# Row tiles of 2 rows by 16 columns in the sums of an involution, with paired weight groups and a ring of 38 rows

## The chip, the cores and the metric

The kernel runs on one core of a Trainium2 chip. The time is the device time of that core in microseconds (us), the median over runs. Durations, waits and rates come from one execution that the hardware profiler recorded. TensorE is PE in the profile (its weight loads are PEld), VectorE is DVE, ScalarE is ACT, GpSimd is POOL and SyncE is SP.

## The reference

Two layers on x of shape (32, 256, 32, 32), each with a group normalization ahead of it and a residual addition behind it. The first is a 3x3 convolution on values rounded to half precision, the second an involution: a 7x7 filter whose 49 weights are computed anew for each pixel and for each of 16 groups of 16 channels.

```python
# layer 0
x = x + (float_quantize(patches3x3(gn(x)) @ weight.T) + bias)      # operands quantized too
# layer 1, on v = gn(x)
y   = relu(bn(einsum('oc,bchw->bohw', w1, v)))                     # 64 channels
w   = einsum('oc,bchw->bohw', w2, y) + b2                          # 16 groups * 49 taps
w   = w.reshape(b, G, K * K, H, W)
out = einsum('bgkhw,bgckhw->bgchw', w, patches7x7(v))              # a filter of its own per pixel and group
x   = x + out
```

## The kernel before

Images go through one after the other, but several are under way at once. The outer loop counts steps `n`; an image takes `per = 16` of them in its last part, the sums. Everything of an image that comes ahead of its sums (both normalizations, the convolution, y, the transposed pixels) is a generator `front(b)` that starts 56 steps earlier and advances a stage in each step. So a step holds stages of some three images' fronts, and in every second step a call of `sums` (L501), `add_windows` (L523) and `weights` (L402). The order on each engine is the order in which the loop writes the instructions (`manual_schedule`); the framework adds the semaphores. In a pair of steps PE runs the sums of one tile, the weights of another image and half a unit of convolution (9 matmuls, L332).

The convolution is done as nine shifted matmuls in float16 for each half of the channels. `weights` computes, for four rows of the image, the 49 filter weights of each pixel and group by float32 matmuls (L410) into two PSUM tiles; DVE adds the bias and writes them into `w_sb` (L428), a ring of 24 rows in SBUF. As the weights of an output pixel have to reach the source pixels around it, an eviction writes the seven rows of taps into seven rows of the ring; where the ring's end or the image's edge cuts a row off, `ring_pieces` (L438) splits the write into several instructions.

`scatter` (L466) writes eight rows of the ring to `wd` in DRAM, one transfer for each column of taps, shifted so that `wd` holds, by source pixel, what that pixel contributes to the window of outputs around it. `load_bands` (L479) fetches from `wd` a band for each tile of 8 rows: 16 transfers, of which POOL issues 14 and SP 2, into one of three band buffers.

In `sums` the source pixels of half a tile are the contraction of a matmul: the pixels (transposed) are the stationary side and the band the moving one. A tile of sums is 4 rows by 16 columns, 64 source pixels; two of them lie in the two halves of PE's rows, and four groups' results in four strips of 32 columns. The result of a tile is a window of 10 rows (`WIN = XR + K1 - 1`) by 19 columns, so 190 columns of PSUM. A call handles two row tiles, two halves of the channels, two groups of a pair and four strips: 32 products. Each float32 product is two weight loads and two matmuls in the profile. `add_windows` (L523) adds the windows to x in SBUF, one instruction for each row tile, written one step after the sums. The accumulators alternate by side: the left and right half of the image have an `acc` each, of two banks.

What the prediction speaks of by line: L332 convolution, L380 y (`py`), L395 transposes (`pt`), L410 weights, L428 their evictions, L477 scatter, L490 bands, L515 sums, L531 additions.

Of the kernel before, what the change touches and what calls it, by code (L numbers as in the profile page):

```python
# [9 lines left out]
F32 = mybir.dt.float32  # L10
AF = mybir.ActivationFunctionType
ALU = mybir.AluOpType

P = 128
B, C, H, W = 32, 256, 32, 32
N = H * W
NT = 512
RT = NT // W
CH = C // P
K0, PAD0 = 3, 1  # L20
K1, PAD1 = 7, 3
TAPS = K1 * K1
CR = 64
G = 16
# [9 lines left out]

XR = 4
RG = 2
KP = P // RG
TR = RG * XR  # L40
SIDES = 2
JC = W // SIDES
K = H // TR
M = K * SIDES
WIN = XR + K1 - 1
WINC = JC + K1 - 1
WINI = JC + PAD1

WB = G * WIN
WPIX = K1 * WB + XR
SW = K1 * G
S = H + 2 * PAD1
T = 4
TW = P // T
PAIR = 3 * GC
PAIRS = G // 2
ROW = S * WPIX  # L60
WR = 4
NBAND = 3
SHARE = 8
NPIX = 6
RING = 24
FRONT = -56
LOAD = -63
LEAD = 18
# [3 lines left out]
def tile_quant_conv_then_involution(  # L72
# [16 lines left out]
    nc = tc.nc  # L89
    PSUM = bass.MemoryType.PSUM  # L90

    const = ctx.enter_context(tc.tile_pool(name="const", bufs=1))
# [45 lines left out]
        nc.gpsimd.memset(t, 0.0)  # L138

    y_sb = [const.tile([P, N // 2], F32, name=f"y_{i}") for i in range(2)]  # L140
    bands = [const.tile([P, SIDES, WINC * WB + XR], F32, name=f"band_{i}") for i in range(NBAND)]
    for t in bands[CH:]:
        nc.gpsimd.memset(t, 0.0)
    pixels = [const.tile([P, 2, PAIRS, PAIR], F32, name=f"pixels_{i}") for i in range(NPIX)]
# [1 line left out]
        nc.gpsimd.memset(t, 0.0)  # L146


    w_sb = const.tile([P, 2, RING, G, WIN], F32, name="w_sb")
    wd = dram.tile([H, S, WPIX], F32, name="wd")  # L150
    acc = [ps_acc.tile([P, RG, NT], F32, name=f"acc_{d}") for d in range(SIDES)]

    wq = const.tile([P, CH, K0 * K0, C], F16, name="wq")
    staged = []
# [4 lines left out]
    w2_sb = const.tile([P, K1, SW], F32, name="w2_sb")  # L159
    for i in range(2):  # L160
        nc.sync.dma_start(w2_sb[i * CR : (i + 1) * CR], w2)
    b2_sb = const.tile([P, 2, SW], F32, name="b2_sb")
    for dj in range(K1):
        t, e = divmod(dj, 2)
        nc.sync.dma_start(b2_sb[t * TW : (t + 1) * TW, e], b2[dj].partition_broadcast(TW))

    bias_sb = const.tile([P, CH], F32, name="bias_sb")
    nc.sync.dma_start(bias_sb, bias0.rearrange("(h p) -> p h", p=P))
# [15 lines left out]


    for col, cols, at, n in (
        (0, S, K1 * WB, XR),
        (PAD1, PAD1, 0, PAD1 * WB),
        (W, PAD1, (K1 - PAD1) * WB, PAD1 * WB),
    ):  # L190
        to = bass.AP(
            tensor=wd.tensor,
            offset=wd.offset + col * WPIX + at,
            ap=[[ROW, H], [WPIX, cols], [1, n]],
        )
        nc.sync.dma_start(to, bands[NBAND - 1][:H, 0, :n].unsqueeze(1).to_broadcast([H, cols, n]))
# [205 lines left out]
    def weights(b, r0):  # L402

        pws = [ps_w.tile([P, 2, 2, SW], F32, tag=f"pw{i}", name=f"pw{i}") for i in range(2)]
        for r in range(2):
            for t in range(T):
                for i in range(2):
                    half = slice(i * CR, (i + 1) * CR)
                    dj = slice(2 * t, min(2 * t + 2, K1))
                    nc.tensor.matmul(  # L410
                        pws[i][t * TW : (t + 1) * TW, r, : dj.stop - dj.start],
                        y_sb[b % 2][half, (r0 // 2 + r) * W : (r0 // 2 + r + 1) * W],
                        w2_sb[half, dj],
                        start=True,
                        stop=True,
                    )
        for i in range(2):
            for e in range(2):
                p = P if e == 0 else (K1 // 2) * TW
                for r, rows, d0, d1, at in ring_pieces(b, r0 + 2 * i):  # L420

                    to = w_sb[:p, e]
                    to = bass.AP(
                        tensor=to.tensor,
                        offset=to.offset + at * WB + K1 - 1 - d0,
                        ap=[to.ap[0], [WB, rows], [WB - 1, d1 - d0], [WIN, G]],
                    )
                    nc.vector.tensor_tensor(  # L428
                        to,
                        pws[i][:p, r : r + rows, e, d0 * G : d1 * G].rearrange("p r (d g) -> p r d g", g=G),  # L430
                        b2_sb[:p, e, d0 * G : d1 * G]
                        .unsqueeze(1)
                        .to_broadcast([p, rows, (d1 - d0) * G])
                        .rearrange("p r (d g) -> p r d g", g=G),
                        ALU.add,
                    )

    def ring_pieces(b, r0):  # L438

        def place(r, d):
            s = r0 + r + d - PAD1
            return (b * H + s) % RING if 0 <= s < H else None

        def together(d):
            return place(0, d) is not None and place(1, d) == place(0, d) + 1

        pieces = []
        for rows, ok in (  # L450
            ((0, 2), together),
            ((0, 1), lambda d: place(0, d) is not None and not together(d)),
            ((1, 1), lambda d: place(1, d) is not None and not together(d)),
        ):
            d = 0
            while d < K1:
                d0 = d
                while d < K1 and ok(d) and place(rows[0], d) == place(rows[0], d0) + d - d0:
                    d += 1
                if d > d0:  # L460
                    pieces.append((*rows, d0, d, place(rows[0], d0)))
                else:
                    d += 1
        return pieces

    def scatter(b, k, part):  # L466

        at = (b * H + k * TR) % RING
        for dj in range(part, K1, 2):
            t, e = divmod(dj, 2)  # L470
            to = bass.AP(
                tensor=wd.tensor,
                offset=wd.offset + k * TR * ROW + dj * WPIX + (K1 - 1 - dj) * WB,
                ap=[[WPIX, TW], [ROW, TR], [1, WB]],
            )
            rows = w_sb[t * TW : (t + 1) * TW, e, at : at + TR]
            nc.sync.dma_start(to, rows.rearrange("p s g r -> p s (g r)"))  # L477

    def load_bands(b, k):  # L479

        band = bands[(b * K + k) % NBAND]
        for i in range(JC):
            j = i // 2 + i % 2 * JC // 2
            src = bass.AP(
                tensor=wd.tensor,
                offset=wd.offset + k * TR * ROW + (j + PAD1) * WPIX,
                ap=[[ROW - 1, TR], [JC * WPIX, SIDES], [1, WPIX]],
            )
            queue = nc.sync if i % SHARE == SHARE - 1 else nc.gpsimd
            queue.dma_start(band[j::JC, :, j * WB : j * WB + WPIX], src)  # L490

    def windows(b, m):


        k, d = divmod(m, SIDES)
        for g in range(RG):
            top = k * TR + g * XR - PAD1
            at = acc[d][:, g, : CH * WINI * WIN].rearrange("p (h j r) -> p h j r", h=CH, r=WIN)
            yield g, at, top, max(top, 0), min(top + WIN, H)

    def sums(b, m):  # L501

        k, d = divmod(m, SIDES)
        j0 = 0 if d else PAD1
        band = bands[(b * K + k) % NBAND][:, d]
        px = pixels[(b * K + k) % NPIX][:, d]
        for h in range(CH):
            for v in range(2):
                for g, at, top, f, l in windows(b, m):
                    p = slice(g * KP, (g + 1) * KP)  # L510
                    of = band[p, g * XR + j0 * WB : g * XR + (j0 + WINI) * WB]
                    of = of.rearrange("p (j g r) -> p j g r", g=G, r=WIN)
                    for t in range(T):
                        a = h * T + t
                        nc.tensor.matmul(  # L515
                            at[t * TW : (t + 1) * TW, h, :, f - top : l - top],
                            px[p, a, v * GC : v * GC + TW],
                            of[:, :, 2 * a + v, f - top : l - top],
                            start=(h, v) == (0, 0),
                            stop=(h, v) == (CH - 1, 1),  # L520
                        )

    def add_windows(b, m):  # L523

        d = m % SIDES
        to = x_tiles[b].rearrange("p h (r c) -> p h r c", c=W)
        j0 = d * (JC - PAD1)
        for g, at, top, f, l in windows(b, m):
            x_at = to[:, :, f:l, j0 : j0 + WINI]
            of = at.rearrange("p h j r -> p h r j")[:, :, f - top : l - top]  # L530
            nc.vector.tensor_tensor(x_at, of, x_at, ALU.add)  # L531
# [10 lines left out]
    def due(n, lag):  # L542

        b, i = divmod(n - lag, per)
        return (b, i) if 0 <= b < B else (None, None)

    with tc.manual_schedule():
        fronts = {}
        for n in range(FRONT, B * per + 2):
            b, i = due(n, FRONT)  # L550
# [12 lines left out]
            b, i = due(n, 0)  # L563
            if b is not None and i % 2 == 0:
                sums(b, i // 2)
            b, i = due(n, 1)
            if b is not None and i % 2 == 0:
                add_windows(b, i // 2)
                if i // 2 == M - 1:
                    store(b, 1)  # L570
                    x_tiles.pop(b)
# [58 lines left out]
```

## Time and profile before

| | |
|---|---|
| median of 3 runs | 1392.44 us (1381.25 to 1393.82) |
| span of the profiled execution, its own time from the first to the last instruction | 1387.9 us |
| first and last start of L515, the sums | 97.4 and 1382.2 us |
| instructions | 70,012 |
| PE busy | 1250.5 us (90%), 29,440 matmuls and 29,440 weight loads |
| DVE busy | 934.7 us (67%) |
| ACT busy | 727.6 us (52%) |
| POOL busy | 1007.6 us (73%) |
| DMA | 369.33 MB in 366,232 packets, mean 266 GB/s |
| mean granted TensorE clock | 0.981 |

The profiled execution has no time of its own other than its span; it lies within the range of the three runs. In the lines below, a group reads: line, engine, operation, out<-in, partitions by elements, count, then busy us and mean ns of one, then the engine's idle time just ahead of it and what ended it. "issue" means that the profile shows nothing that the engine waited for. A row of the timeline reads: start us, length us, and what ran. The DMA row has a digit for each fortieth of the span, in tenths of the 16 engines.

### The profile page before, as it was taken

The numbers are of one execution on the slowest core, as the hardware profiler recorded it, in microseconds if no ns is written. First come the engines' busy times: TensorE is split into PE (matmuls) and PEld (weight loads), VectorE is DVE, ScalarE is ACT, GpSimd is POOL, SyncE is SP. The second block draws the span as 40 slices with busy tenths as digits, with TensorE's granted clock in tenths as the row PEclk, the third lists the DMA queues.
The fourth block names the chain that finished last, engine by engine and source line by source line (L and its number), as shares of the span: only waits on it lengthen the run. The fifth ranks groups of instructions, "written<-read, shape, count | busy, mean of one in ns | idle before, by whom it ended". The sixth has DMA issues, their size and how long they took to land.

```text
span 1387.9 us, 70012 instructions
## 1 busy us (share of the span) xinstructions
PE 1250.5 (90%) x29440; PEld 798.5 (58%) x29440; DVE 934.7 (67%) x3179; ACT 727.6 (52%) x1699; POOL 1007.6 (73%) x1818
## 2 busy tenths in 40 slices
PE   2899999899899999998899999899999999999665
PEld 1356555566565665655565666566566655666543
DVE  4467776677767776776576677667777776677652
ACT  4866555465645555655455555545565654653300
POOL 8057777777787777767777787776876777778785
PEclk9999999999999999999999999999999999999986
DMA  6079999999999998999999999999999999999995
GB/s 217 1 195 286 283 277 283 284 266 292 287 277 274 287 294 254 285 279 269 273 275 286 289 275 279 288 277 264 288 283 272 295 285 279 280 280 272 280 269 162
DMA packets 366232, 369.33 MB, mean 266 GB/s; under 512 B 78624, under 2 KB 308192, under 8 KB 365664
## 3 DMA queue, kind: packets, MB, share of 16 engines
q1 hardware_dynamic: 279904, 235.72, 57.5%
q0 software_dynamic: 86016, 129.14, 33.8%
q8 instruction: 234, 3.83, 1.2%
q14 instruction: 78, 0.64, 0.1%
HBM read 183.81 MB, written 180.74 MB: 263 GB/s over the span
## 4 chain that ended last, share of the span: by engine, by line
PE 55%; DMA 25%; DVE 5%; issue 5%; POOL 4%; SPq 3%; ACT 3%; POOLq 0%; DVEq 0%; ACTq 0%
PE pc L332 22%; PE acc L515 17%; DMA band<-wd 14%; PE pw L410 10%; DMA wd<-w_sb 8%; POOL band L490 4%; PE py L380 3%; DVE w_sb L428 3%; SPq L477 3%; PE pt L395 2%; DMA out<-x 1%; ACT junk L219 1%; DVE x L531 1%; DMA band<-in_w 1%; ACT xn L278 0%
## 5 line engine op out<-in xcount | busy, mean ns | idle before, releaser
L490 POOL DMA_DIRECT2D band<-wd x1792 | 978.0, 548 | 364.1 <-DMA band<-wd 225.3
L428 DVE TENSOR_TENSOR w_sb<-pw,b_sb 128x16 f32<-128x16 f32 (+9 forms) x1920 | 455.5, 349 | 359.2 <-PE pw L410 345.4
L332 PE MATMUL pc<-xq,wq 128*128 128x496 f16 (+3 forms) x2304 | 536.4, 379 | 32.5 <-ACT xq L278 28.0
L515 PE MATMUL acc<-band,pixels 64*32 64x190 f32 (+1 forms) x16384 | 411.6, 322 | 80.2 <-DMA band<-wd 44.6
L332 PEld LDWEIGHTS <-wq 128*128 128x128 f16 x2304 | 206.8, 98 | 328.2 <-issue 113.0
L515 PEld LDWEIGHTS acc<-band,pixels 64*32 64x32 f32 x16384 | 296.1, 108 | 165.1 <-issue 100.1
L410 PE MATMUL pw<-w_sb,y 64*32 64x224 f32 (+1 forms) x8192 | 291.2, 332 | 15.1 <-issue 13.9
L531 DVE TENSOR_TENSOR x<-acc,x 128x380 f32<-128x380 f32 (+1 forms) x512 | 261.7, 511 | 33.6 <-PE acc L515 24.6
L410 PEld LDWEIGHTS pw<-w_sb,y 64*32 64x32 f32 x8192 | 180.6, 106 | 45.7 <-issue 28.8
L399 ACT COPY pixels<-pt 128x512 f32<-128x512 f32 x128 | 73.6, 575 | 224.0 <-PE pt L395 224.0
L219 ACT ACTIVATE junk<-x 128x512 f16<-128x512 f32 (+1 forms) x192 | 146.5, 763 | 18.0 <-DVE x L348 9.6
L219 ACT ACTIVATE junk<-x,mean 128x1024 f16<-128x1024 f32 x128 | 147.1, 1149 | 4.3
L250 ACT ACTIVATE s<-back,eps 128x2 f32<-128x2 f32 x64 | 18.9, 296 | 207.3 <-DVE back L235 207.2
L346 DVE TENSOR_SCALAR q<-pc 128x512 f16<-128x512 f32 x128 | 87.2, 682 | 19.2 <-PE pc L332 19.0
L278 ACT ACTIVATE xn<-x,off,rstd 128x512 f32<-128x512 f32 x128 | 96.1, 800 | 0.0
L348 DVE SCALAR_TENSOR_TENSOR x<-q,bias_sb,x 128x512 f32<-128x512 f16 x128 | 92.0, 719 | 0.2
L395 PEld LDWEIGHTS pt<-ident,xn 128*128 128x128 f32 x512 | 63.9, 142 | 27.7 <-issue 3.3
L395 PE MATMUL pt<-ident,xn 128*128 128x128 f32 x512 | 78.0, 275 | 1.5 <-ACT pixels L399 1.5
L240 ACT ACTIVATE mean<-back 128x2 f32<-128x2 f32 x64 | 12.7, 198 | 120.6 <-DVE back L235 120.6
L278 ACT ACTIVATE xq<-x,off,rstd 128x1024 f16<-128x1024 f32 x64 | 75.5, 1226 | 0.0
L380 PEld LDWEIGHTS py<-xn,w_sb 128*64 128x64 f32 x2048 | 62.7, 138 | 16.7 <-issue 8.3
L380 PE MATMUL py<-xn,w_sb 128*64 128x64 f32 x2048 | 67.5, 224 | 2.8 <-ACT xn L278 1.8
(40 smaller groups left out, 374.5 us busy)
## 6 DMA issues: line engine op xcount, KB each, us to landing
wd<-w_sb SPq DMA_DIRECT2D x896, 160.0 KB
band<-wd POOLq DMA_DIRECT2D x1792, 70.2 KB, 4.9
x<-in_x SPq DMA_DIRECT2D x64, 512.0 KB
out<-x SPq DMA_DIRECT2D x64, 512.0 KB
band<-wd SPq DMA_DIRECT2D x256, 70.2 KB
band<-in_w SPq DMA_DIRECT2D x2, 1152.0 KB
w_sb<-in_w SPq DMA_DIRECT2D x2, 196.0 KB
wd<-band SPq DMA_DIRECT2D x2, 180.0 KB
```

Of the source, the lines that this page charges most:

```text
L219: nc.scalar.activation(junk[:, n0:n1], src[:, h, n0:n1], func, bias=bias, accum_out=self.sums[:, i : i + 1])
L278: nc.scalar.activation(dst, src, AF.Identity, bias=self.off[:, one], scale=self.rstd[:, one])
L332: nc.tensor.matmul(pc.rearrange("p (r c) -> p r c", c=W)[:, r0 - nt * RT : r1 - nt * RT, c0:c1], wq[:, kh, k, mh * P : (mh + 1) * P], xq[: ...
L346: nc.vector.tensor_scalar(q, pc, F16_MAX, -F16_MAX, ALU.min, ALU.max)
L348: nc.vector.scalar_tensor_tensor(xt[:, mh, cols], q, bias_sb[:, mh : mh + 1], xt[:, mh, cols], ALU.add, ALU.add)
L380: nc.tensor.matmul(py[i * CR : (i + 1) * CR, cols], w1_sb[:, kh, :], px[:, r : r + 2], start=kh == 0, stop=kh == CH - 1,)
L395: nc.tensor.transpose(pt[:, i, h * P : (h + 1) * P], xn[:, h, (m + i) * P : (m + i + 1) * P], ident)
L410: nc.tensor.matmul(pws[i][t * TW : (t + 1) * TW, r, : dj.stop - dj.start], y_sb[b % 2][half, (r0 // 2 + r) * W : (r0 // 2 + r + 1) * W], w ...
L428: nc.vector.tensor_tensor(to, pws[i][:p, r : r + rows, e, d0 * G : d1 * G].rearrange("p r (d g) -> p r d g", g=G), b2_sb[:p, e, d0 * G : d ...
L490: queue.dma_start(band[j::JC, :, j * WB : j * WB + WPIX], src)
L515: nc.tensor.matmul(at[t * TW : (t + 1) * TW, h, :, f - top : l - top], px[p, a, v * GC : v * GC + TW], of[:, :, 2 * a + v, f - top : l - top],
L531: nc.vector.tensor_tensor(x_at, of, x_at, ALU.add)
```

## The change

A tile of sums becomes 2 rows by 16 columns (`XR = 2`), and four of them (`RG = 4`) lie in the four quarters of PE's rows with 32 source pixels each. The window shrinks to 8 rows, 152 columns of PSUM, and a call has 64 products. Each row tile has an accumulator bank of its own, `acc[g]`, which both sides share. `add_windows` has four instructions of 8-row windows, and is called right behind `sums` in the same step.

The weights are laid out in pairs of groups (`V = 2`, `A = 8`): the two groups of a pair are neighbours in `w_sb`, in `wd` and in the bands, and w2 and b2 are permuted on the host to match. A pixel's row in `wd` holds 7 x 128 values and a pad of 12 (before 7 x 160 and 4).

The ring has 38 rows, an image's 32 and three on either side, at fixed places. So an eviction always writes all seven rows of taps, those outside the image too, in one instruction of two image rows by 16 groups by 7 taps; `ring_pieces` goes. The matmuls of `weights` write with the tap column ahead of the row, and the bias is held twice, once for each of the two rows.

```diff
-XR = 4
-RG = 2
+XR = 2
+RG = 4
...
+V = 2
+A = G // V
 WB = G * WIN
-WPIX = K1 * WB + XR
+PAD = V * (TR - XR)
+WPIX = K1 * WB + PAD
...
-RING = 24
+RING = H + 2 * PAD1
...
-    w_sb = const.tile([P, 2, RING, G, WIN], F32, name="w_sb")
+    w_sb = const.tile([P, 2, RING, A, WIN, V], F32, name="w_sb")
-    acc = [ps_acc.tile([P, RG, NT], F32, name=f"acc_{d}") for d in range(SIDES)]
+    acc = [ps_acc.tile([P, NT], F32, name=f"acc_{g}") for g in range(RG)]
...
-    b2_sb = const.tile([P, 2, SW], F32, name="b2_sb")
+    b2_sb = const.tile([P, 2, 2, SW], F32, name="b2_sb")
     for dj in range(K1):
         t, e = divmod(dj, 2)
-        nc.sync.dma_start(b2_sb[t * TW : (t + 1) * TW, e], b2[dj].partition_broadcast(TW))
+        for r in range(2):
+            nc.sync.dma_start(b2_sb[t * TW : (t + 1) * TW, e, r], b2[dj].partition_broadcast(TW))
...
-                        pws[i][t * TW : (t + 1) * TW, r, : dj.stop - dj.start],
+                        pws[i][t * TW : (t + 1) * TW, : dj.stop - dj.start, r],
...
-                for r, rows, d0, d1, at in ring_pieces(b, r0 + 2 * i):
...
+                evict(pws[i][:p, e], e, 0, 2, 0, K1, r0 + 2 * i)
+
+    def evict(of, e, r, rows, d0, d1, at):
+
+        p = of.shape[0]
+        to = w_sb[:p, e]
+        to = bass.AP(
+            tensor=to.tensor,
+            offset=to.offset + at * WB + V * (K1 - 1 - d0),
+            ap=[to.ap[0], [V * WIN, rows * A], [WB - V, d1 - d0], [1, V]],
+        )
+        of = of.rearrange("p r (a d v) -> p (r a) d v", a=A, v=V)
+        bias = b2_sb[:p, e, r : r + rows].rearrange("p r (a d v) -> p (r a) d v", a=A, v=V)
+        nc.vector.tensor_tensor(to, of[:, :, d0:d1], bias[:, :, d0:d1], ALU.add)
...
-        at = (b * H + k * TR) % RING
+        at = k * TR + PAD1
...
-                ap=[[ROW - 1, TR], [JC * WPIX, SIDES], [1, WPIX]],
+                ap=[[ROW - V, TR], [JC * WPIX, SIDES], [1, WPIX]],
...
-            at = acc[d][:, g, : CH * WINI * WIN].rearrange("p (h j r) -> p h j r", h=CH, r=WIN)
+            at = acc[g][:, : CH * WINI * WIN].rearrange("p (h j r) -> p h j r", h=CH, r=WIN)
...
-                    of = band[p, g * XR + j0 * WB : g * XR + (j0 + WINI) * WB]
-                    of = of.rearrange("p (j g r) -> p j g r", g=G, r=WIN)
+                    of = band[p, V * g * XR + j0 * WB : V * g * XR + (j0 + WINI) * WB]
+                    of = of.rearrange("p (j a r v) -> p j a r v", a=A, r=WIN, v=V)
...
-                            of[:, :, 2 * a + v, f - top : l - top],
+                            of[:, :, a, f - top : l - top, v],
...
                 sums(b, i // 2)
+                add_windows(b, i // 2)
             b, i = due(n, 1)
             if b is not None and i % 2 == 0:
-                add_windows(b, i // 2)
                 if i // 2 == M - 1:
                     store(b, 1)
```

More of the change, by code (lines that the diff above doesn't have):

```diff
@@ L140, in tile_quant_conv_then_involution @@
     y_sb = [const.tile([P, N // 2], F32, name=f"y_{i}") for i in range(2)]
-    bands = [const.tile([P, SIDES, WINC * WB + XR], F32, name=f"band_{i}") for i in range(NBAND)]
+    bands = [const.tile([P, SIDES, WINC * WB + PAD], F32, name=f"band_{i}") for i in range(NBAND)]
     for t in bands[CH:]:
@@ L186, in tile_quant_conv_then_involution @@
     for col, cols, at, n in (
-        (0, S, K1 * WB, XR),
+        (0, S, K1 * WB, PAD),
         (PAD1, PAD1, 0, PAD1 * WB),
@@ L419, in weights @@
                 p = P if e == 0 else (K1 // 2) * TW
-                for r, rows, d0, d1, at in ring_pieces(b, r0 + 2 * i):
[L422 to L464, printed above, removed]
+                evict(pws[i][:p, e], e, 0, 2, 0, K1, r0 + 2 * i)
@@ L476, in scatter @@
             rows = w_sb[t * TW : (t + 1) * TW, e, at : at + TR]
-            nc.sync.dma_start(to, rows.rearrange("p s g r -> p s (g r)"))
+            nc.sync.dma_start(to, rows.rearrange("p s a r v -> p s (a r v)"))
     def load_bands(b, k):
@@ L603 @@
     v = {name: np.asarray(a) for name, a in inputs.items()}
-    w2 = v["L1_conv_w2"].reshape(G, K1, K1, CR).transpose(3, 2, 1, 0).reshape(CR, K1, K1 * G)
-    b2 = v["L1_conv_b2"].reshape(G, K1, K1).transpose(2, 1, 0).reshape(K1, K1 * G)
+    w2 = v["L1_conv_w2"].reshape(A, V, K1, K1, CR).transpose(4, 3, 0, 2, 1).reshape(CR, K1, K1 * G)
+    b2 = v["L1_conv_b2"].reshape(A, V, K1, K1).transpose(3, 0, 2, 1).reshape(K1, K1 * G)
     laid_out = {
```

## The prediction

> **What bounds the kernel now.** I read the busy shares and the slices first, then the DMA queues, the chain, the groups of instructions, the waits, and last PE's timeline.
>
> ```profile
> PE 1250.5 (90%) x29440; PEld 798.5 (58%) x29440; DVE 934.7 (67%) x3179; ACT 727.6 (52%) x1699; POOL 1007.6 (73%) x1818
> ...
> DMA  6079999999999998999999999999999999999995
> ...
> q1 hardware_dynamic: 279904, 235.72, 57.5%
> q0 software_dynamic: 86016, 129.14, 33.8%
> q8 instruction: 234, 3.83, 1.2%
> ...
> PE 55%; DMA 25%; DVE 5%; issue 5%; POOL 4%; SPq 3%; ACT 3%; POOLq 0%; DVEq 0%; ACTq 0%
> ```
>
> Two resources are nearly full at once: PE at 90%, DMA at nine tenths or more in nearly every slice. The small line is q8: 234 packets, 3.83 MB, so 16,384 bytes each. The trace lists 60,041 instructions of PE (weight loads, matmuls, waits); by 64 bytes that is 3.84 MB. So q8 is PE's own program, in blocks of 256 instructions.
>
> ```profile
> L515 PE MATMUL acc<-band,pixels 64*32 64x190 f32 x12288 | 409.2, 332 | 60.9 <-DMA band<-wd 33.7 <-issue 14.8 <-DMA wd<-w_sb 5.0
> L515 PEld LDWEIGHTS acc<-band,pixels 64*32 64x32 f32 x16384 | 296.1, 108 | 165.1 <-issue 100.1 <-DVE x L531 22.9 <-DVE q L346 12.2
> L531 DVE TENSOR_TENSOR x<-acc,x 128x380 f32<-128x380 f32 x384 | 207.8, 541 | 26.1 <-PE acc L515 19.4
> L428 DVE TENSOR_TENSOR w_sb<-pw,b_sb 128x224 f32<-128x224 f32 x256 | 142.0, 555 | 166.0 <-PE pw L410 162.5 <-DMA wd<-w_sb 3.4
> ```
>
> The reader is to see the counts and "issue": the sums run 16,384 weight loads and as many matmuls, two of each per float32 product, and the largest idle time before them (100.1 us) has no releaser at all.
>
> ```profile
> 664.80 1.49 PE L515 MATMUL acc<-band,pixels 64*32 64x190 f32 x64
> 666.00 1.04 PE L410 MATMUL pw<-w_sb,y 64*32 64x224 f32 x32
> 666.97 2.08 PE L332 MATMUL pc<-xq,wq 128*128 128x496 f16 x9
> ...
> 684.11 1.47 PE L515 MATMUL acc<-band,pixels 64*32 64x190 f32 x50
> 687.61 0.48 PE L515 MATMUL acc<-band,pixels 64*32 64x190 f32 x8 [2.02 <-issue]
> ```
>
> First three lines: the undisturbed step, sums 1.3, weights 0.9, convolution 2.0 us from start to start. Last two: the same sums torn apart after 50 of 64 matmuls by 2.02 us of "issue". I looked up what stands behind it. With PE's instructions numbered by time, 47 of the 216 blocks between 100 and 1300 us end in a stop of more than 0.4 us (45 us together), at a number that leaves 193 on division by 256, and nearly all stops at that place end 1.1 to 1.6 us after a q8 packet landed. So PE runs one block ahead at most: the fetch of the next block starts when a block is entered, and PE stands if it uses 256 instructions up faster than a fetch takes. From the first instruction of a block to the start of its successor's packet: 2.33 us mean; the packet 1.11 us; from landing to the resumed PE, where it stood, about 1.4 us. Together 4.8 us. PE today uses a block in 5.5 us, hardly more.
>
> That start delay follows the load of the DMA engines in the same stretch: about 0.8 us at 30 to 60% busy, 1.0 at 60 to 80%, 1.7 at 80 to 90%, 2.2 to 2.9 above 90%.
>
> [...] In the trace half-clock windows of 3.41 us begin at 270, 523, 628 and 895 us, each after a window in which PE was busy 23 to 44%.
>
> **The change part by part.** The sum is made against the profiled execution, span 1387.9 us (4.5 under the median 1392.4). Sums run from 97.4 to 1382.2 us: 1284.8 / 32 = 40.15 us an image, 97.4 ahead and 5.7 behind.
>
> *Tiles of 2 rows.* Twice as many tiles: 32 products a call become 64, so L515 has 32,768 weight loads and matmuls each. On the array: a matmul of 190 columns starts 161 ns after its predecessor in the same tile (trace), eight in a row, 1.3 us a call. With 152 columns 161 x 0.8 = 129, eight in a row 1.03 us, if sixteen 32x32 tiles run side by side. This is nowhere shown; where weight loads came singly the trace has 16 ns a product, so 64 x 16 = 1.03 us too, but 16 ns for each of 128 loads would be 2.1 us. Bounds per image: 8 x -0.27 = -2 us to 8 x +0.8 = +6 us. I take 1.2 us a call, -1 us.
>
> *Instructions.* PE's 60,041 become 92,800; per image 1,876 become 2,900, that is 7.33 blocks become 11.33. This is on the path. One call of sums is now 256 instructions, a whole block in 1.2 us; PE's own work per image is 8 x (1.2 + 0.9 + 2.0) + 2.0 (py) + 4 x 0.55 (pt) = 37 us, 3.3 us a block, below 4.8. So nearly every block waits for its fetch.
>
> *Traffic.* A band packet shrinks from 4496 to 3632 bytes, a scatter packet from 640 to 512. The trace's packets sum per engine to 495 us for bands, 517 for scatter, 270 for the rest. Bands by bytes: 400. Scatter: between 414 (by bytes) and 517 (a fixed cost per packet). With 9 for more fetches: 1093 to 1196 us, 34 to 37 us an image, against 40.06 now. DMA is then no longer full: at 46 us an image 74 to 80%. The start delay is then between 1.0 and 1.7, I take 1.35. A block: 1.35 + 1.1 + 1.4 = 3.85 us, ends 3.3 (0.8) and 4.8 (no relief).
>
> *The sum.* 11.33 x 3.85 = 43.6 us. Blocks whose own work is longer add the excess: the one with py (weights 0.9, conv 2.0, py 2.0, some sums: 5.1) and some with pt, together +1.5. A block with nothing but sums leaves PE idle 2.6 us, which resembles what came ahead of the half-clock windows; one such window an image costs some 1.2 us. 46.3 us an image: 97.4 + 32 x 46.3 + 5.7 = 1584.7, less 11 since the last nine calls have no weights beside them (0.33 block x 3.85 each): 1574. With the 4.5 between span and median, and rounded: **1578 us**.
>
> *DVE.* Evictions: 1,920 become 1,024 of 224 elements. Their durations sum to 643 us now; at 555 ns it is 568, and 384 if writing pairs side by side reaches the pace of the additions (from 266 to 380 elements, 421 to 541 ns, 1.05 ns each). I take 568. Additions: 512 become 1,024; 304 elements by the same slope are 461 ns, 421 and 341 at the edges, mean 441, 452 us against 262. DVE gains at most 115 us and may lose 69; at 67% it stays beside PE. Cost nothing, covered by PE.
>
> *Order and buffers.* The additions stand one step earlier on DVE, and the accumulators no longer alternate: a call must wait for all additions of the call before. Four take 1.8 us; weights and convolution between the calls take 2.9. Cost nothing; without this cover up to some 0.5 us a call, 4 an image. The early wait holds up the evictions behind it, but these wait for matmuls that PE runs after the sums. At worst today's waits on L531 (22.9 + 6.0 us) double: +29. I take nothing, since a fetch stop gives DVE time.
>
> *Ring of 38 rows, doubled bias.* Evictions meet their scatters later (13.4 us of waits on them now): 0 to -13, beside PE. The order of SP and POOL is unchanged; seven more bias loads on SP at about 0.6 us each push the small loads behind them 4 us, long before weights at 64 us. The memset of the ring grows by a quarter of 6.5 us, those of the bands shrink. Nothing.
>
> **The rivals.** *Freed:* fetches come in below 3.2 us once DMA is at ease; PE needs 36 to 37 us an image, and DMA's 34 to 37 lets it. 97 + 32 x 37 + 6 = **1287 us, faster**. For it: DMA is full now (POOL's bands wait 225 us on earlier bands), and relieved by 11 to 15%. Against: even at half load I read 0.8 + 1.1 + 1.4 = 3.3 us, and at 37 us an image DMA would be 92% busy again, where a fetch takes 4.7. It decides where the whole fetch is under about 3.2 us. *Slow loading:* fetches hide, yet small weight loads go one after the other, 2.1 us a call: 44 us an image, **1510 us**. Against: starts 5 to 7 ns apart in different tiles. *No relief:* a block stays at 4.8 us: 54.5 us an image, **1843 us**. *Balance:* the fetch costs what DMA gives back, 40 us, **1390 us**. That the tiles wouldn't shrink is excluded: the built program has 16,384 products at 152 columns or fewer.
>
> **How the numbers follow.** Fetch-paced with some relief 0.72 (own ends: 3.3 us a block with long blocks as they are, 42 us an image, 1440; 4.4 us, 51 us, 1730); no relief 0.07; slow loading 0.08; freed 0.10; balance 0.03. Range 1440 to 1740, which leaves out freed, balance and no relief. Faster by over 1% 0.10, within 1% (about what a measurement can tell) 0.03, slower 0.87.
>
> **What would show it.** Right: about 362 packets on q8; "issue" before L515 and L410 in the hundreds of us; PE's share below 80% with its work hardly grown; DMA's tenths at 7 to 8; undisturbed sums of about 1.2 us; stops at one place modulo 256. Wrong: DMA tenths at 9 with PE waiting on bands (traffic bounds), sums of 2 us without a stop (loading), or PE waiting on L504's additions (hand-over).

## The result, and the profile after

The changed kernel takes **1816.73 us** in the median of 4 runs (1810.38 to 1821.39), against 1391.51 us for the kernel before beside it: a ratio of 1.305, 95% interval 1.300 to 1.309. It is slower, as forecast, but by 425 us instead of 186, and the time lies beyond the range of 1440 to 1740. The profiled execution has a span of 1819.6 us.

From the page of the changed kernel: busy shares, clock and DMA in 40 slices, queues, the chain.

```profile
PE 1557.6 (86%) x45824; PEld 923.1 (51%) x45824; DVE 1034.0 (57%) x2795; ACT 730.8 (40%) x1699; POOL 1019.1 (56%) x1818
...
PEclk9999999999899999999999999999999999999875
DMA  5376666666667656666666675666666567666664
...
q1 hardware_dynamic: 280240, 202.89, 37.9%
q0 software_dynamic: 57344, 104.37, 23.9%
q8 instruction: 362, 5.93, 1.4%
...
PE 82%; issue 12%; ACT 2%; DVE 2%; POOL 1%; DMA 1%; SPq 0%; DVEq 0%; ACTq 0%; POOLq 0%
```

DMA has dropped from nine tenths to six and out of the chain (25% to 1%); PE with "issue" is 94% of it. q8 has the 362 packets that were forecast: PE's program has grown by half, 60,041 to 92,808 instructions, which is 257 and 256 to a packet.

The groups of the changed kernel that answer to those shown of before, by form:

```profile
L488 PE MATMUL acc<-band,pixels 32*32 32x152 f32 x24576 | 572.7, 306 | 85.9 <-issue 82.8 <-DVE back L239 1.5 <-DVE x L504 0.5
L488 PEld LDWEIGHTS acc<-band,pixels 32*32 32x32 f32 x32768 | 431.4, 105 | 267.1 <-issue 164.9 <-DVE w_sb L437 27.3 <-DVE x L504 17.9
L504 DVE TENSOR_TENSOR x<-acc,x 128x304 f32<-128x304 f32 x768 | 364.5, 475 | 392.9 <-PE acc L488 329.8 <-issue 3.4 <-DVE x L504 2.3
L437 DVE TENSOR_TENSOR w_sb<-pw,b_sb 128x224 f32<-128x224 f32 x512 | 195.3, 382 | 93.0 <-PE pw L414 92.4
```

The largest idle time ahead of the sums is again "issue". And from its waits (who waited for whom: us in total, times, longest):

```profile
POOL band L463 <- PE acc L488: 321.7, 62, 9.1
...
PEld L336 <- issue: 200.6, 495, 6.9
...
PEld acc L488 <- issue: 164.9, 201, 4.1
PEld pw L414 <- issue: 124.2, 124, 4.7
PE acc L488 <- issue: 113.8, 92, 3.8
```

The bands now wait for PE to give their buffers back (321.7 us), where they waited on earlier bands before (225 us). The roles have turned round: DMA is early, PE late.

The timeline of PE in the changed kernel, twice:

```profile
906.46 2.02 PE L488 MATMUL acc<-band,pixels 32*32 32x152 f32 x128
908.40 0.97 PE L414 MATMUL pw<-w_sb,y 64*32 64x224 f32 x32
909.31 2.08 PE L336 MATMUL pc<-xq,wq 128*128 128x512 f16 x9
911.32 2.01 PE L488 MATMUL acc<-band,pixels 32*32 32x152 f32 x128
913.26 0.37 PE L414 MATMUL pw<-w_sb,y 64*32 64x224 f32 x1
917.10 1.85 PE L414 MATMUL pw<-w_sb,y 64*32 64x224 f32 x31 [3.46 <-issue]
918.88 3.94 PE L336 MATMUL pc<-xq,wq 128*128 128x496 f16 x9
```

Three things are to be seen. An undisturbed call of the sums takes 1.94 us from its start to that of the weights (906.46 to 908.40), where it took 1.3. Then PE stands for 3.46 us with nothing to wait for. And after that the weights take 1.85 us instead of 0.97 and the convolution 3.94 instead of 2.08: the granted clock is at half from 916.0 to 922.8 us.

An image takes 53.71 us (sums from 94.4 to 1813.1 us), 13.56 more than the 40.15 of before. Three terms, each from the traces of both kernels, over the stretch of the sums:

| | before | after | difference |
|---|---|---|---|
| undisturbed call of the sums, window not cut by the image's edge, at full clock, start to start of what follows (median) | 1.31 us | 2.00 us | 0.69 us, by 256 calls 177 us |
| PE's stops at a block's end (instruction numbers that leave 193 on division by 256): distances of two starts over 0.4 us, less 0.1 us each; number and sum | 49, 48 us | 166, 258 us | +210 us |
| windows at half clock that begin in this stretch, and half of PE's busy time in them | 48, 20 us | 250, 113 us | +93 us |

The three make 480 us where the span grew by 432. The rest came back elsewhere, by the 45 us for instance that the sums waited on bands before and no longer do; calls at the image's edge and pieces at half clock also overlap between rows. The table is an account of where the time lies. It does not say that one row would go away by itself: the experiments show that less in one row can mean more in another.

### The profile page after: what moved, and what is told of

The parts are those of the page before. It is cut to its first block, busy times and chain, and to the rows that moved or that the text cites. A ratio compares the mean times of both kernels' runs of the same rounds, so it can differ in the third digit from the quotient of the medians.

```text
span 1819.6 us, 103269 instructions
## 1 busy us (share of the span) xinstructions
PE 1557.6 (86%) x45824; PEld 923.1 (51%) x45824; DVE 1034.0 (57%) x2795; ACT 730.8 (40%) x1699; POOL 1019.1 (56%) x1818
## 4 chain that ended last, share of the span: by engine, by line
PE 82%; issue 12%; ACT 2%; DVE 2%; POOL 1%; DMA 1%; SPq 0%; DVEq 0%; ACTq 0%; POOLq 0%
PE acc L488 31%; PE pc L336 29%; PE pw L414 15%; PE py L384 3%; PE pt L399 3%; ACT junk L223 1%; DVE x L504 1%; POOL band L206 1%; DVE w_sb L437 0%; DMA x<-in_x 0%; DMA wd<-w_sb 0%; POOL pixels L149 0%; POOL band L146 0%; ACT xn L282 0%; DMA band<-wd 0%
## 5 line engine op out<-in xcount | busy, mean ns | idle before, releaser
L463 POOL DMA_DIRECT2D band<-wd x1792 | 988.9, 555 | 777.8 <-PE acc L488 321.7
L504 DVE TENSOR_TENSOR x<-acc,x 128x304 f32<-128x304 f32 (+2 forms) x1024 | 465.7, 455 | 546.6 <-PE acc L488 463.7
L488 PE MATMUL acc<-band,pixels 32*32 32x152 f32 (+2 forms) x32768 | 596.4, 302 | 117.5 <-issue 113.8
L336 PE MATMUL pc<-xq,wq 128*128 128x496 f16 (+3 forms) x2304 | 589.1, 405 | 49.8 <-ACT xq L282 24.6
L488 PEld LDWEIGHTS acc<-band,pixels 32*32 32x32 f32 x32768 | 431.4, 105 | 267.1 <-issue 164.9
L336 PEld LDWEIGHTS <-wq 128*128 128x128 f16 x2304 | 217.9, 103 | 393.3 <-issue 200.6
L437 DVE TENSOR_TENSOR w_sb<-pw,b_sb 128x224 f32<-128x224 f32 (+1 forms) x1024 | 326.4, 380 | 93.0 <-PE pw L414 92.4
L414 PE MATMUL pw<-w_sb,y 64*32 64x224 f32 (+1 forms) x8192 | 297.8, 355 | 83.2 <-issue 81.0
L414 PEld LDWEIGHTS pw<-w_sb,y 64*32 64x32 f32 x8192 | 144.7, 111 | 180.9 <-issue 124.2
```

The lines of the kernel that those rows point to most:

```text
L336: nc.tensor.matmul(pc.rearrange("p (r c) -> p r c", c=W)[:, r0 - nt * RT : r1 - nt * RT, c0:c1], wq[:, kh, k, mh * P : (mh + 1) * P], xq[: ...
L414: nc.tensor.matmul(pws[i][t * TW : (t + 1) * TW, : dj.stop - dj.start, r], y_sb[b % 2][half, (r0 // 2 + r) * W : (r0 // 2 + r + 1) * W], w ...
L437: nc.vector.tensor_tensor(to, of[:, :, d0:d1], bias[:, :, d0:d1], ALU.add)
L488: nc.tensor.matmul(at[t * TW : (t + 1) * TW, h, :, f - top : l - top], px[p, a, v * GC : v * GC + TW], of[:, :, a, f - top : l - top, v], ...
```

## The experiments

Theory A is that of the prediction: PE's number of instructions sets the time, since blocks of 256 come one ahead. The other letters are named in the expectations.

**The instructions alone.** In the kernel before, each product of the sums is cut in two by columns.

```diff
-                    for t in range(T):
...
-                            at[t * TW : (t + 1) * TW, h, :, f - top : l - top],
...
-                            of[:, :, 2 * a + v, f - top : l - top],
-                            start=(h, v) == (0, 0),
-                            stop=(h, v) == (CH - 1, 1),
+                    for j in (slice(0, 10), slice(10, WINI)):
+                        for t in range(T):
...
+                                at[t * TW : (t + 1) * TW, h, j, f - top : l - top],
...
+                                of[:, j, 2 * a + v, f - top : l - top],
+                                start=(h, v, j.start) == (0, 0, 0),
+                                stop=(h, v, j.start) == (CH - 1, 1, 10),
```

> The kernel before, with each product of the sums cut into two of 10 and 9 columns of the window: the same array work, traffic, layout and additions, twice the instructions in the sums (PE 60,041 to about 92,800). Theory A (PE's instruction count sets the time, by blocks of 256 that are fetched one ahead): 11.33 blocks an image at 4.8 us or more, since DMA is still full: 54 us an image, 1750 to 1900 us. Theory B (the loss of the change lies in the new tiles' layout, evictions, bands or additions): 1390 us, within 2%.

Measured: 1840.1 us, ratio 1.320 (1.316 to 1.325). With the layout, the traffic, the evictions and the additions of before, twice the instructions in the sums cost as much as the whole change. There are stops of 362 us and 215 us at half clock. The undisturbed calls grew as well, from 1.31 to 1.77 us (median of 65), with the same columns in all. From its timeline (100 and 90 columns in a matmul):

```profile
1004.93 0.58 PE L516 MATMUL acc<-band,pixels 64*32 64x100 f32 x30
1005.96 1.50 PE L516 MATMUL acc<-band,pixels 64*32 64x90 f32 x96 [0.45 <-issue]
```

A call is torn apart after about 30 of its 128 matmuls without a releaser, as in the kernel before, but now in 212 of 356 blocks. Theory B falls.

**Half of the products.** The changed kernel without the second group of each pair.

```diff
-            for v in range(2):
+            for v in range(1):
...
-                            stop=(h, v) == (CH - 1, 1),
+                            stop=(h, v) == (CH - 1, 0),
```

> The changed kernel without the second group of each pair in the sums (half of the products are left out; traffic, evictions and additions stay). PE's instructions fall back to about 60,000. Theory A: 7.33 blocks an image of 4.4 us are 32 us, less than PE's own work of 8 x (1.0 + 0.9 + 2.0) + 4.2 = 35.4; 36 to 38 us an image, 1260 to 1330 us. Theory B (additions, hand-over of the accumulators, bands): still above 1600 us.

Measured: 1341.24 us, ratio 0.963 (0.958 to 0.967). A little above the expected stretch, and far from B's. With 60,040 instructions the stops are 54 us. All the rest of the change is still in it, so that rest does not slow this kernel down. The array work of the sums is halved here too; the narrow window below takes that part alone away.

**The two parts by themselves.** First the tile size with its accumulators on the kernel before, without pairing and without the long ring:

```diff
-XR = 4
-RG = 2
+XR = 2
+RG = 4
...
-WPIX = K1 * WB + XR
+PAD = TR - XR
+WPIX = K1 * WB + PAD
...
-    acc = [ps_acc.tile([P, RG, NT], F32, name=f"acc_{d}") for d in range(SIDES)]
+    acc = [ps_acc.tile([P, NT], F32, name=f"acc_{g}") for g in range(RG)]
...
-            at = acc[d][:, g, : CH * WINI * WIN].rearrange("p (h j r) -> p h j r", h=CH, r=WIN)
+            at = acc[g][:, : CH * WINI * WIN].rearrange("p (h j r) -> p h j r", h=CH, r=WIN)
...
+                add_windows(b, i // 2)
             b, i = due(n, 1)
             if b is not None and i % 2 == 0:
-                add_windows(b, i // 2)
```

> The kernel before with the tile size alone: 2 rows, four accumulators shared by both sides, additions right behind the sums; weights not paired, ring of 24 rows, evictions in pieces. Theory A: the same 92,800 instructions, so the time of the changed kernel, 1780 to 1850 us. Theory B1 (pairing or the ring of 38 rows carries the loss): below 1600 us.

Measured: 1800.26 us, ratio 1.290 (1.283 to 1.296). The tile size carries the loss. Then the pairs alone, on tiles of 4 rows (shown against the changed kernel; `ring_pieces` is that of before):

```diff
-XR = 2
-RG = 4
+XR = 4
+RG = 2
...
-RING = H + 2 * PAD1
+RING = 24
...
-                evict(pws[i][:p, e], e, 0, 2, 0, K1, r0 + 2 * i)
+                for r, rows, d0, d1, at in ring_pieces(b, r0 + 2 * i):
+                    evict(pws[i][:p, e, r : r + rows], e, r, rows, d0, d1, at)
...
-        at = k * TR + PAD1
+        at = (b * H + k * TR) % RING
...
-                add_windows(b, i // 2)
             b, i = due(n, 1)
             if b is not None and i % 2 == 0:
+                add_windows(b, i // 2)
```

> The other part alone: weights in pairs of groups and evictions in pairs, with tiles of 4 rows, alternating accumulators, late additions and the ring of 24 rows as before. Theory A: PE's instructions as before, so 1375 to 1405 us; the lighter evictions of DVE (380 instead of 555 ns) may give a per cent. Theory B1: above 1450 us.

> The same kernel of the paired weights with tiles of 4 rows as before, beside the more even order and in more rounds: 0.985 to 0.995 of the kernel before.

Measured: 1380.31 us, ratio 0.990 (0.987 to 0.994), and again 1380.9 us, 0.990 (0.986 to 0.993). This part is a per cent faster than the kernel before, the fastest version found that computes all. Its evictions are shorter:

```profile
L438 DVE TENSOR_TENSOR w_sb<-pw,b_sb 128x224 f32<-128x224 f32 x256 | 98.2, 383 | 192.3 <-PE pw L414 185.7 <-DMA wd<-w_sb 6.5
```

383 ns for the 555 of before. DVE's busy time falls by 73 us, but DVE waits for PE there, so this is not shown to be what the 11 us come from; in the trace the sums begin 4 us earlier and an image takes 39.9 or 40.0 us instead of 40.15. That stays open.

**What a fetch waits for.** The changed kernel with short band transfers; what is not loaded is missing from the sums.

```diff
-                ap=[[ROW - V, TR], [JC * WPIX, SIDES], [1, WPIX]],
+                ap=[[ROW - V, TR], [JC * WPIX, SIDES], [1, WB]],
...
-            queue.dma_start(band[j::JC, :, j * WB : j * WB + WPIX], src)
+            queue.dma_start(band[j::JC, :, j * WB : j * WB + WB], src)
```

> The changed kernel with band transfers of 128 instead of 908 values per pixel (most of the bands stays unloaded, so the sums add only part). Instructions and all else as changed. Theory A: the fetch of a block waits behind data on the DMA engines; with about half of the traffic gone the start delay falls from 1.85 towards 1.1 us, a block from 4.4 to 3.6, below PE's own 3.8 to 3.9 us a block: stops fall from 258 us to under 130, half-clock time with them, 44 to 48 us an image, 1500 to 1640 us; the undisturbed sums stay at 1.95 us. Theory D (the fetch takes as long whatever DMA carries): 1780 us or more.

Measured: 1668.82 us, ratio 1.201 (1.192 to 1.211). The DMA slices:

```profile
DMA  5154554445545445544444544454454455544442
```

Theory D falls: with less on the DMA engines the start of a fetch comes 1.45 us after its block is entered instead of 1.85, the stops fall from 258 to 163 us and the half-clock time from 250 to 142. The time is 148 us shorter. That is less than A expected: the delay has a part that does not go, and stops remain in more than a third of the blocks. The undisturbed calls stay at 2.00 us.

**Why a call takes 2 us.** The changed kernel with the first 10 columns of the window in sums and additions.

```diff
-                            at[t * TW : (t + 1) * TW, h, :, f - top : l - top],
+                            at[t * TW : (t + 1) * TW, h, :10, f - top : l - top],
...
-                            of[:, :, a, f - top : l - top, v],
+                            of[:, :10, a, f - top : l - top, v],
...
-            x_at = to[:, :, f:l, j0 : j0 + WINI]
-            of = at.rearrange("p h j r -> p h r j")[:, :, f - top : l - top]
+            x_at = to[:, :, f:l, j0 : j0 + 10]
+            of = at.rearrange("p h j r -> p h r j")[:, :, f - top : l - top, :10]
```

> The changed kernel with sums and additions of the first 10 of 19 columns of the window alone (9 columns are left out): as many instructions, half of the array work. On why an undisturbed call takes 1.95 us where the array needs 1.03: theory W (PE holds 64 instructions, 16 products, at a time, and the next ones enter as these retire, some 0.48 us a round, of which two matmuls of 127 ns are part): 4 x 0.36 = 1.4 to 1.5 us. Theory S (weight loads or dispatch one after the other, 15 ns a pair): unchanged 1.95 us. The whole time: fetches still rule, 1650 to 1780 us by W, by S 1780 or more.

Measured: 1830.47 us, ratio 1.317 (1.308 to 1.327), and undisturbed calls of 1.52 us (median of 73, all 80 columns wide). From its timeline:

```profile
907.47 1.56 PE L488 MATMUL acc<-band,pixels 32*32 32x80 f32 x128
908.96 0.98 PE L414 MATMUL pw<-w_sb,y 64*32 64x224 f32 x32
```

On the call, S falls: at a fixed 15 ns a pair its length would not depend on the columns. At the pace of before (161 ns for 190 columns) a matmul of 72 columns less is 61 ns shorter; the call is 481 ns shorter, about eight times as much. So eight matmuls lie one behind the other in a call, two in each of four rounds, and what they leave over is 2002 - 8 x 129 = 970 ns, 0.24 us a round. The trace of the changed kernel shows the rounds: in the call at 906.46 us the first 64 instructions start within 0.23 us, and the next rounds begin at 906.93, 907.41 and 907.88, each as matmuls of the round before end. That agrees with W; that it is a limit of 64 is inferred from that count. Whether the small tiles themselves make a call longer was not tried apart. Against it speaks the kernel with the cut products: it has the eight larger tiles of before, and its calls are 0.46 us longer for the same columns (1.77 for 1.31). On the whole time W was wrong and S's number right for another reason. The calls gave up 0.48 us each, some 120 us in all; what they gave up went into the stops (339 us) and half clock (391 us). **Taking half of the array work out of the sums saved nothing.**

**The hand-over.** The additions one step later, as before.

```diff
                 sums(b, i // 2)
-                add_windows(b, i // 2)
             b, i = due(n, 1)
             if b is not None and i % 2 == 0:
+                add_windows(b, i // 2)
```

> The changed kernel with the additions put back where they were, one step later. Theory A: DVE's additions have room between two calls of the sums (PE waits 18 us on them), so within 1% of the changed kernel, 1800 to 1835 us. Theory H (the early wait at the head of DVE's queue holds up evictions and so PE): 1740 us or less.

Measured: 1934.84 us, ratio 1.394 (1.387 to 1.400). Both numbers were missed. From its waits:

```profile
PEld acc L488 <- DVE x L504: 332.4, 809, 2.6
...
PE acc L488 <- DVE x L504: 65.4, 87, 1.8
```

PE now waits 398 us for the additions. In that place they stand behind what the fronts of the next step give DVE, which waits for convolution of that same step; with accumulators that do not alternate, the next sums wait for them. So the early place costs little, as forecast (PE waits 18 us for the additions there), but it is not free to choose: it saves 118 us.

**The order of PE's work.** The changed kernel with its pieces more evenly mixed.

```diff
-    CONV = (9, 0, 9, 0)
+    CONV = (5, 4, 5, 4)
...
-    def sums(b, m):
+    def sums(b, m, h):
...
-                sums(b, i // 2)
-                add_windows(b, i // 2)
+                sums(b, i // 2, 0)
             b, i = due(n, 1)
             if b is not None and i % 2 == 0:
+                sums(b, i // 2, 1)
+                add_windows(b, i // 2)
```

> The changed kernel with the same instructions in another order: the sums of the two channel halves in two successive steps, and the convolution in 5 and 4 matmuls a step instead of 9 and 0, so that the blocks of 256 instructions take more equal times. Theory A: PE stops where a block's own work is shorter than its fetch; blocks of some 3.8 us each with fetches of 4.4 give 11.33 x 4.4 = 50 us an image, and fewer half-clock windows: 1640 to 1740 us. Theory N (the stops depend only on the number of instructions, as if the fetch were a mean rate): unchanged, 1800 us or more.

Measured: 1762.47 us, ratio 1.269 (1.262 to 1.276), that is 54 us less than the changed kernel. The stops fall from 258 to 57 us with the same matmuls and weight loads, and the half-clock time from 250 to 131: theory N falls. Uneven blocks belong to the cause of the stops. In the changed kernel a tenth of the blocks takes under 2.2 us from its first start to its last and half of them over 4.3; here these are 3.6 and 4.3. The fetches start sooner as well, 1.45 us after their block is entered instead of 1.85, and this run does not separate the two. The time fell less than A expected, for a new wait came, that of the hand-over:

```profile
PEld acc L487 <- DVE x L503: 217.3, 538, 1.3
```

**The same order on the faster kernel.** The kernel of the pairs alone, with the convolution in 5 and 4 and the weights moved between the calls.

```diff
-    CONV = (9, 0, 9, 0)
+    CONV = (5, 4, 5, 4)
...
-            b, i = due(n, -LEAD)
+            b, i = due(n, -LEAD - 1)
             if b is not None and i % 2 == 0:
                 weights(b, i // 2 * WR)
```

> The kernel of the paired weights with tiles of 4 rows, with PE's pieces in a more even order: 5 and 4 matmuls of the convolution in successive steps instead of 9 and 0, and the weights moved to the step between two calls of the sums. Theory A (stops come from blocks that are used up faster than they are fetched): the 42 us of stops fall below 25 and the time to 1350 to 1372 us. Theory P (DMA bounds this kernel, its slices stand at nine tenths, so what PE saves it waits for bands): 1372 to 1385 us, with longer waits on bands.

Measured: 1394.74 us, ratio 1.002 (1.000 to 1.005). The stops fell from 52 to 10 us, an image takes 40.0 us as before, and neither number was met; it is slower than the same kernel in the old order. Its DMA slices:

```profile
DMA  6089999999999999999999999999999999999995
```

With tiles of 4 rows DMA stands at nine tenths in both orders, and taking out most of the stops did not shorten an image. This speaks for DMA as the bound of that kernel; it was not tried by taking DMA work out of that kernel.

## Why the prediction was right or wrong

**The sign and the cause: right.** The fetch of PE's instructions, one block ahead, was read out of the profile of before. The splitting, the halving, the tile size by itself and the shorter bands confirm it. In each of the 356 blocks of the changed kernel PE enters the next block 1.07 us or more after its packet landed, and 166 of the 356 crossings stop PE. The count (362 packets), the "issue" in hundreds of us and the place of the stops came as described, and the rival *freed* fell. Two signs did not come: PE's share is 86% and not below 80%, as its calls grew longer and part of its work ran at half clock, and DMA stands at six tenths and not at 7 to 8.

**The step that failed: the price of a fetch.** I took 3.85 us for a block, with a start delay of 1.35. Measured are 1.85 us for the delay, 1.16 for the packet and 1.4 for the resumption, so 4.4 us. In the prediction's own sum 0.55 us by 11.33 blocks is 6.2 us an image, some 200 us of the 239 by which the time exceeds the forecast. That the time follows this price is what the short bands show: there a fetch takes 3.97 us, the calls stay as they are, and the kernel is 148 us faster. It is not that its bands come sooner: the changed kernel's sums have no wait for a band. And the five kernels with as many matmuls and weight loads and without the new wait for the additions stand in the order of their fetches: short bands 3.97 us a fetch and 1669 us in all, tile size alone 4.34 and 1800, the change 4.40 and 1817, narrow window 4.41 and 1830, cut products 4.54 and 1840.

The delay came from a table by DMA load, read at a mean load. In the kernel before only 12 of 228 blocks had DMA less than 80% busy between their entry and the landing of their packet, so the lower rows of the table rest on little. And the changed kernel's 63% is a mean of bursts: 182 of 356 blocks met DMA over 80% busy, with a mean delay of 2.25 us, and 57 met it under 10% busy, with 1.13 us still. The table also mixed two kinds of blocks: the 179 of the kernel before that were entered without a stop read shorter (2.14 us) than the 49 entered with one (2.89 us).

**Nearly every block waits: wrong.** 190 of 356 do not; these take 4.89 us of their own, the other 166 take 4.74, where my sum has 4.1 for each. That my sum leaves 46.3 - 37 - 1.2 = 8.1 us of stops in an image and the trace has 258 / 32 = 8.1 is luck: with the shorter calls of the narrow window there are 339 / 32 = 10.6.

**The length of a call of sums: mis-sized as well.** I gave bounds of 1.03 and 2.1 us, took 1.2, and it is 2.0. On paper 0.8 us by eight calls, 6.4 us an image, would fill the gap too. But the narrow window took 0.48 us of that away and the time did not fall, so as far as this run goes the calls are not where the time was lost. The mechanism that I gave for the upper bound (loads one after the other) is wrong; the trace shows rounds of 64 instructions, 16 products, begun 0.47 to 0.48 us apart.

**The clock: right in kind, too small.** I put one half-clock window to an image at 1.2 us. There are 250 us of them, 45 us in one piece at the end, and 113 us of lost pace, 3.5 us an image. That is some 74 us more than I allowed; it is not independent of the fetch, since the short bands brought it down with the stops (250 to 142 us). My upper end, 4.4 us a block, gave 1730 us, and most of the 87 us from there can be put down to this. The start of the windows is not tied to the 44% that I read as the upper end: all but the last follow a window in which PE was busy 63% or less, and several of these were over 50%.

**What was costed at nothing.** DVE: evictions at 382 ns, the lower of my two ends, and additions of 304 elements at 475 ns for my 461; its busy time rose from 934.7 to 1034.0 us, beside PE. Hand-over: PE waits 18 us before its loads on L504. Ring, bias, memsets: the sums begin at 94.4 us instead of 97.4. DMA: 63% of the span in its three queues for my 74 to 80%, because the image is longer. The relief of DMA that I put at 11 to 15% is 7 to 15% by my own sums; the packets' time per engine fell by 10%.

## What to carry to other kernels

Count PE's instructions in blocks of 256 (here 60,041 came in 234 packets, 92,808 in 362) and compare the time in which the densest block is used up with what a fetch takes (here 4.4 us with DMA at 63%, 4.8 with DMA full). Take the delay at the DMA load that the fetches meet (here 2.25 us over 80% busy, 1.13 us under 10%), and not at the mean of the span. The small tiles of float32 products brought many instructions for little array work (92,808 for 60,041): what they were to save on the array and in traffic came back as stops (258 us for 48), and more half clock came with the stops (250 us, and 142 us where the stops fell to 163). Where a profile shows "issue" inside a block of equal instructions on PE, look for this before counting columns.

## What the runs showed of the hardware

A call of 64 float32 products on sixteen 32x32 tiles took 2.00 us with 152 columns and 1.52 us with 80: at the pace of 161 ns for 190 columns that is 8 matmuls one behind the other and some 0.97 us over in both. Nearly halving the columns left the kernel at 1830 us for 1817: here less array work brought more stops (339 us for 258) and more time at half clock (391 us for 250). And with the same number of elements DVE's evictions took 383 ns instead of 555 where two neighbours in the destination are written together instead of every tenth element; the order of reading changed with it. Writing every eighth element instead, in the kernel with the tile size alone, took 563 ns.
